# A graph network and attention kernel: the last sigmoid by the hyperbolic tangent, with its sum on another engine

## The chip, the cores and the metric

The kernel runs on one core of one Trainium2 chip. A core has five engines with a queue each, which run side by side and wait for one another by semaphores: TensorE (PE, matrix products, with its weight loads shown as PEld), VectorE (DVE), ScalarE (ACT), GpSimd (POOL) and SyncE (SP), which here only issues transfers. Within an engine the instructions run in the order in which they stand. The metric is the time of one execution on the device in microseconds (us); lower is better.

## The reference

The input x has 128 graphs of 128 nodes with 256 features, adj one weight matrix of 128 x 128 for each graph. Two layers follow, each behind a layer norm and a rectifier. Layer 0 is a graph product with a bias; layer 1 is attention with eight heads whose logits are sums of a q and a k, one number for each node and head:

```python
h = jnp.maximum(_layernorm(x, axis=-1), 0.0)
x = x + (adj @ (h @ weight) + bias)            # layer 0
h = jnp.maximum(_layernorm(x, axis=-1), 0.0)
logits = q + jnp.swapaxes(k, -1, -2)           # q, k = (h @ fc_w + fc_b) @ q_w, k_w
masked = jax.nn.leaky_relu(logits + (1.0 - adj) * NEG, negative_slope=0.01)
attn = jax.nn.softmax(masked, axis=-1)
out = (attn @ feat_proj) @ fp_w + fp_b + h     # heads side by side
x = x + jax.nn.sigmoid(out)                    # layer 1
```

All is in fp32. Two identities stand behind the change: sigmoid(z) = 0.5 tanh(z / 2) + 0.5, and a layer norm takes away any constant that is added to all features of a node.

## The kernel before

The 128 graphs are taken in 32 groups of 4. The nodes lie on the 128 partitions; a tile of a group's features is 128 x 1024. A loop over the groups has 44 slots each. In every slot PE gets one piece of work, by a fixed list of 11 (ORDER, L595) that is gone through once for each of the group's four units (two pairs of graphs, two halves of the heads): `aggregate` (L561) multiplies attention with features into PSUM, and `multiply` (L599) multiplies seven sums and differences of the unit before, f0 to f6, with weights that hold fc_w and fp_w together. `take` (L572) makes f0 to f6: f0, f1 and f3 are copies on ACT (L581, L589, L583), f4 and f6 sums on DVE (L585, L586), f5 and f2 differences on POOL (L587, L590). `combine` (L617) adds the products up into the tile z on DVE.

All other work is put into the slots by the list PLAN (L673), written out by hand: a slot, a group relative to the loop's (-1 is the group before, 1 the next), a function. Since every engine has a queue in that order, PLAN sets what stands in front of what. The functions that the change and the prediction touch:

- The attention of the next group: `masked` (slots 0, 5, 12) spreads k over a tile and adds the mask on DVE (L489, L497); `leaky` is eight ACT instructions for each graph (L510), `head_max` a reduction on DVE (L518), `exps` eight ACT instructions with sums (L526), `normal` a reciprocal on DVE (L534) and the product with it on POOL (L535); `move` issues SP's transfers (L546) that exchange blocks of 32 partitions, and `turn` transposes within the blocks on DVE (L553).
- `make_qk` (slot 24) computes q and k of the group after next on PE (L453) and adds their bias on DVE (L461). `turn_qk` (slot 27) transposes them on PE (L467), copies k and q out on DVE (L469, L471) and issues k to memory on SP (L473); `load_k` (slot 34) brings it back on all partitions (L478).
- Layer 0 of the group three ahead: `n1_stats` (slot 28) and `n1_apply` (slot 25) are its norm on DVE and ACT (L285, L319); `add_b0` (slot 29) adds the bias to x on POOL (L337), after `n1_apply` has read it; `first_a` and `first_b` (slots 35 to 40) are its products, and `first_b` adds x in two halves on DVE into the tile x1 (L390), on which `n2_stats` follow.
- The end of the group before: `residual_a` and `residual_b` add h on POOL (L648, L653), `sigmoid` (slot 28) runs on ACT, `finish` (slot 29) adds x1 on POOL, `store` (slot 34) issues the result on SP.

ACT has its functions in tables. Prelu, exp, the rectifier and copies run with one table here, sigmoid with another; the loads between them carry the line of the instruction that needs them.

Of the kernel before, what the change touches and what calls it, by code (L numbers as in the profile page):

```python
# [10 lines left out]
AF = mybir.ActivationFunctionType  # L11
ALU = mybir.AluOpType
# [16 lines left out]
def gnn_then_gat_kernel(  # L29
# [16 lines left out]
    nc = tc.nc  # L46
# [38 lines left out]
    nc.sync.dma_start(w0_sb, w0.rearrange("(c p) o -> p c o", p=P))  # L85
    b0_bc = const.tile([P, D], FP, name="b0_bc")
    nc.sync.dma_start(b0_bc, b0.partition_broadcast(P))
    fpb_j = const.tile([P, D], FP, name="fpb_j")


# [559 lines left out]
    def residual_b(s, pair):  # L650
        for b in range(2 * pair, 2 * pair + 2):
            z = s["z"][:, b].rearrange("p (c j q) -> p j c q", j=NB, q=Q)
            nc.gpsimd.tensor_tensor(z, z, s["h2"][:, b], ALU.add)  # L653

    def sigmoid(s, b0, nb):
        z = s["z"][:, b0 : b0 + nb]
        nc.scalar.activation(z, z, AF.Sigmoid)  # L657

    def finish(s, b0, nb):
        bs = slice(b0, b0 + nb)  # L660
        nc.gpsimd.tensor_tensor(s["z"][:, bs], s["z"][:, bs], s["x1"][:, bs], ALU.add)  # L661

    def store(s, b0, nb):
        bs = slice(b0, b0 + nb)
# [55 lines left out]
        (25, 3, n1_apply, 1),  # L720
        (27, "u", combine, 1, 4),
        (28, "u", take, 2, 1, 0),
        (27, 2, turn_qk),
        (28, 1, move, 0, range(8, 16)),
        (28, 1, normal, 3),
        (28, 3, turn_blocks),
        (28, 4, n1_stats, 0),
        (28, 4, n1_stats, 1),
        (28, -1, sigmoid, 0, GB),
        (29, -1, finish, 0, GB),  # L730
        (29, 3, add_b0),
        (30, 1, move, 1, range(6)),
# [173 lines left out]
    for g in range(NG):  # L906
        cur = groups[g]
        cur["z"] = pool["un"].tile([P, GB, D], FP, name="z", tag="z")
        last = units[-1]
        units = [{"s": cur, "pair": i // 2, "half": i % 2, "f": {}} for i in range(4)]  # L910
        for slot in range(4 * len(ORDER)):
            n, i = divmod(slot, len(ORDER))
            o = ORDER[i]
            if isinstance(o, tuple):
                aggregate(units[n], o[1], o[2])
            elif n or last:
                multiply(units[n - 1] if n else last, o)
            if g == 0:
                for at_, f, *args in FIRST_PLAN:
                    if at_ == slot:  # L920
                        f(*args)
            for at_, who, f, *args in PLAN:
                if at_ != slot or (g == 0 and f in LATE):
                    continue
                if who == "u":
                    u = last if args[0] < 0 else units[args[0]]
                    if u:
                        f(u, *args[1:])
                elif g + who in range(NG):
                    f(groups[g + who], *args)  # L930
            if g == NG - 1 and slot == 33:
                sigmoid(cur, 0, 2)
            if g == NG - 1 and slot == 35:
                finish(cur, 0, 2)
                store(cur, 0, 2)
    for o in ORDER:
        if not isinstance(o, tuple):
            multiply(units[3], o)
            combine(units[3], o)
    residual_b(cur, 1)  # L940
    sigmoid(cur, 2, 2)
    finish(cur, 2, 2)
    store(cur, 2, 2)

# [30 lines left out]
```

## Time and profile before

| | us |
|---|---|
| median of 3 runs | 1575.77 (1575.29 to 1577.64) |
| the profiled execution, its own time | 1576.38 |
| its span, first to last instruction | 1574.2 |

| engine | busy us | share of the span |
|---|---|---|
| PE | 1509.0 | 96% |
| DVE | 1228.9 | 78% |
| ACT | 1173.8 | 75% |
| POOL | 984.0 | 63% |

| group of instructions | count | mean us of one |
|---|---|---|
| table loads at L657 (sigmoid) | 30 | 1.283 |
| table loads at L526 (exp) | 30 | 1.283 |
| L657 ACT, sigmoid of a group | 31 | 1.057 |
| L661 POOL, the sum with x1 of a group | 31 | 2.377 |
| L337 POOL, the sum of x and the bias | 32 | 2.360 |
| L390 DVE, x1 by halves | 64 | 0.690 |
| L467 PE, the turn of q and k | 32 | 0.33 |

The profile is one execution. A span is the time from the first to the last instruction on the core; the execution's own time has some 2 us around it. Busy time of PE is modelled, since products overlap; where PE is concerned, starts of instructions are the surer measure. A timeline lists instructions in order of time with their start and length, and in brackets the idle time before one and the instruction that ended it.

### The profile page before, as it was taken

Reading aid. Unit: us, or ns where it says so; the run is one execution under the profiler, and the core shown is the slowest. Engines: PE = TensorE matmul, PEld = TensorE weight load, DVE = VectorE, ACT = ScalarE, POOL = GpSimd, SP = SyncE. Lnnn points to the kernel's source line nnn. Section 1 sums busy time; section 2 is a strip of 40 time slices with the busy share of each in tenths; the row PEclk is TensorE's granted clock in tenths of the full one; section 3 lists DMA queues with packets and bytes.
Section 4 is the critical chain, followed back from the end, with each engine's and each line's share of the span. In section 5 each row is a group of like instructions: output and inputs, shape, how many; then the busy total and the mean of one; then the engine's idle time right before and its main releaser. Section 6 shows DMA issues by size and latency. Waiting matters only on the chain.

```text
span 1574.2 us, 30745 instructions
## 1 busy us (share of the span) xinstructions
PE 1509.0 (96%) x9953; PEld 1213.2 (77%) x9953; DVE 1228.9 (78%) x2253; ACT 1173.8 (75%) x3889; POOL 984.0 (63%) x724
## 2 busy tenths in 40 slices
PE   7786999999999999999999999999999999999997
PEld 7565877887777878777777877777877777778776
DVE  5676778887777888777888877788887778887762
ACT  3683788777778877777987777897777789777751
POOL 3163766666676666676666667666666766666664
PEclk7888999999999999999999999999999999999999
DMA  5132434434444443444444344444434444433320
GB/s 181 34 88 63 104 84 97 94 90 88 101 93 97 95 93 78 102 104 90 97 93 95 80 102 105 87 98 92 94 82 101 107 83 98 92 78 80 73 68 27
DMA packets 259689, 142.07 MB, mean 90 GB/s; under 512 B 174901, under 2 KB 226505, under 8 KB 259273
## 3 DMA queue, kind: packets, MB, share of 16 engines
q1 hardware_dynamic: 259288, 139.79, 39.7%
q8 instruction: 78, 1.28, 0.4%
q14 instruction: 83, 0.67, 0.2%
q10 hardware_dynamic: 240, 0.33, 0.1%
HBM read 39.86 MB, written 17.30 MB: 36 GB/s over the span
## 4 chain that ended last, share of the span: by engine, by line
ACT 44%; PE 23%; DVE 16%; SPq 9%; issue 4%; DMA 2%; POOL 2%; ACTq 0%; POOLq 0%; DVEq 0%
ACT attn L526 18%; PE acc L609 11%; ACT attn L510 10%; SPq L546 6%; DVE attn L497 6%; ACT h L319 6%; PE x_ps L383 5%; PE g_ps L564 5%; DVE attn L489 5%; ACT f L589 2%; ACT L657 2%; ACT L526 2%; SPq L426 2%; ACT z L657 2%; DVE st L285 1%
## 5 line engine op out<-in xcount | busy, mean ns | idle before, releaser
L609 PEld LDWEIGHTS acc<-wts,f 128*128 128x128 f32 x7168 | 889.6, 192 | 281.2 <-issue 181.7
L609 PE MATMUL acc<-wts,f 128*128 128x128 f32 x7168 | 897.9, 276 | 23.8 <-DVE z L625 12.9
L564 PE MATMUL g_ps<-attnT,h 128*128 128x512 f32 x1024 | 530.1, 600 | 5.3 <-DVE attnT L553 3.3
L526 ACT ACTIVATE attn<-attn,nmax 128x128 f32<-128x128 f32 x1024 | 397.3, 396 | 0.4
L587 POOL TENSOR_TENSOR f<-f,f 128x512 f32<-128x512 f32 x128 | 163.2, 1275 | 286.7 <-DVE f L585 284.4
L510 ACT ACTIVATE attn<-attn,q 128x128 f32<-128x128 f32 x1024 | 312.9, 391 | 34.4 <-DVE attn L497 27.1
L535 POOL TENSOR_TENSOR attn<-attn,total 128x1024 f32<-128x1024 f32 x128 | 245.1, 1915 | 140.8 <-DVE total L534 140.8
L589 ACT COPY f<-g_ps 128x512 f32<-128x512 f32 x128 | 73.3, 572 | 241.1 <-PE g_ps L564 241.1
L518 DVE TENSOR_REDUCE nmax<-attn 128x8 f32<-128x1024 f32 x128 | 154.0, 1204 | 64.1 <-ACT attn L510 63.9
L526 ACT ACTIVATION_READ_ACCUMULATOR attn<-attn,nmax 128x1 f32 x1024 | 199.3, 195 | 0.0
L497 DVE TENSOR_TENSOR attn<-attn,mask 128x1024 f32<-128x1024 f32 x128 | 186.4, 1456 | 4.5
L590 POOL TENSOR_TENSOR f<-f,f 128x512 f32<-128x512 f32 x128 | 180.5, 1410 | 6.5 <-ACT f L589 3.9
L553 DVE STREAM_TRANSPOSE attnT<-attnB 128x1024 f32<-128x1024 f32 x128 | 153.3, 1218 | 39.7 <-DMA attnB<-attn 34.7
L489 DVE STREAM_TRANSPOSE attn<-kq 128x1024 f32<-128x1024 f32 x128 | 157.2, 1228 | 15.9 <-DMA kq<-k_mem 15.6
L564 PEld LDWEIGHTS g_ps<-attnT,h 128*128 128x128 f32 x1024 | 157.6, 194 | 13.8 <-issue 9.6
L383 PE MATMUL x_ps<-w_sb,ahT 128*128 128x256 f32 x512 | 124.2, 387 | 0.0
L585 DVE TENSOR_TENSOR f<-g_ps,f 128x512 f32<-128x512 f32 x128 | 87.1, 681 | 47.3 <-POOL attn L535 38.9
L661 POOL TENSOR_TENSOR z<-z,x 128x1024 f32<-128x1024 f32 (+1 forms) x33 | 76.2, 2310 | 56.3 <-ACT z L657 56.3
L653 POOL TENSOR_TENSOR z<-z,h 128x256 f32<-128x256 f32 x128 | 90.7, 731 | 23.3 <-DVE z L625 22.7
L581 ACT COPY f<-g_ps 128x512 f32<-128x512 f32 x128 | 74.0, 578 | 40.7 <-PE g_ps L564 39.6
L383 PEld LDWEIGHTS x_ps<-w_sb,ahT 128*128 128x128 f32 x512 | 93.5, 192 | 11.6 <-issue 0.7
L586 DVE TENSOR_TENSOR f<-f,g_ps 128x512 f32<-128x512 f32 x128 | 86.5, 676 | 0.0
(93 smaller groups left out, 1356.8 us busy)
## 6 DMA issues: line engine op xcount, KB each, us to landing
attnB<-attn SPq DMA_DIRECT2D x1019, 64.0 KB, 2.0
xg<-in_x_dram SPq DMA_DIRECT2D x32, 512.0 KB, 4.0
out_dram<-z SPq DMA_DIRECT2D x31, 512.0 KB, 3.1
h2B<-h SPq DMA_DIRECT2D x480, 32.0 KB, 1.9
ag<-in_adj_dram SPq DMA_DIRECT2D x32, 256.0 KB, 4.5
agB<-in_adj_dram SPq DMA_DIRECT2D x120, 64.0 KB, 4.5
fcw<-in_L_gnn_fc_w_dram SPq DMA_DIRECT2D x2, 1024.0 KB, 6.9
fpw<-in_L_gnn_fp_w_dram SPq DMA_DIRECT2D x1, 2048.0 KB, 14.1
```

The source lines that it names most:

```text
L383: nc.tensor.matmul(op[:, bb, :], lhsT=s["ahT"][:, 2 * b2 + bb, c, :], rhs=w0_sb[:, c, :], start=(c == 0), stop=(c == NC - 1),)
L489: nc.vector.transpose(s["a", b // 2][:, :, b % 2], s["kq"][:, :, b].unsqueeze(3).to_broadcast([P, NB, H, Q]),)
L497: nc.vector.tensor_tensor(a, a, s["mask"][:, b, :] .rearrange("p (j c) -> p j c", c=Q) .unsqueeze(2) .to_broadcast([P, NB, H, Q]), ALU.add,)
L510: nc.scalar.activation(a[:, :, h, :], a[:, :, h, :], AF.Prelu, bias=s["q"][:, b, h : h + 1], alpha=0.01,)
L518: nc.vector.tensor_reduce(nmax, a.rearrange("p j h c -> p h j c"), AX.XY, ALU.max, negate=True)
L526: nc.scalar.activation(a[:, :, h, :], a[:, :, h, :], AF.Exp, bias=s["nmax", b][:, h : h + 1], accum_out=s["total", b][:, h : h + 1],)
L535: nc.gpsimd.tensor_tensor(a, a, total.unsqueeze(1).unsqueeze(3).to_broadcast([P, NB, H, Q]), ALU.mult)
L553: nc.vector.transpose(aT.rearrange("p h (i r) -> p i h r", r=Q), s["ab", b // 2][:, :, b % 2])
L564: nc.tensor.matmul(u["g", b, c], lhsT=s["h2"][:, 2 * pair + b].rearrange("p j c q -> p (j c q)")[:, ts(c, P)], rhs=s["aT", 2 * pair + b][: ...
L587: nc.gpsimd.tensor_tensor(new(5), f[4], f[0], ALU.subtract)
L590: nc.gpsimd.tensor_tensor(new(2), f[1], f[5], ALU.subtract)
L609: nc.tensor.matmul(acc[:, slot, :], lhsT=u["f"][m][:, h, :], rhs=wt[m][:, half * HU + h, :], start=(half == 0 and h == 0 and m in FIRST), ...
```

## The change

Sigmoid becomes a hyperbolic tangent of half its argument. Its half factor is applied where x1 is added, in one instruction with two operations, which stands on DVE instead of POOL. Its half summand is added once, at the start, to the bias of layer 0, on POOL: so x1 is larger by 0.5 everywhere, the norm of layer 1 takes that away again, and the last sum has it. In PLAN, `turn_qk` goes from slot 27 to slot 28 and stands there behind `take`, so on PE behind the aggregation of slot 28.

```diff
     b0_bc = const.tile([P, D], FP, name="b0_bc")
     nc.sync.dma_start(b0_bc, b0.partition_broadcast(P))
+    nc.gpsimd.tensor_scalar(b0_bc, b0_bc, 0.5, None, ALU.add)
...
     def sigmoid(s, b0, nb):
         z = s["z"][:, b0 : b0 + nb]
-        nc.scalar.activation(z, z, AF.Sigmoid)
+        nc.scalar.activation(z, z, AF.Tanh, scale=0.5)
 
     def finish(s, b0, nb):
         bs = slice(b0, b0 + nb)
-        nc.gpsimd.tensor_tensor(s["z"][:, bs], s["z"][:, bs], s["x1"][:, bs], ALU.add)
+        nc.vector.scalar_tensor_tensor(
+            s["z"][:, bs], s["z"][:, bs], 0.5, s["x1"][:, bs], ALU.mult, ALU.add
+        )
...
         (27, "u", combine, 1, 4),
         (28, "u", take, 2, 1, 0),
-        (27, 2, turn_qk),
+        (28, 2, turn_qk),
         (28, 1, move, 0, range(8, 16)),
```

The SP, PE and ACT queues keep their order but for that step of PE and the table loads, which follow from the functions; DVE has one instruction more for each group, behind `n1_stats` and ahead of `combine`.

## The prediction

> **What bounds the kernel now.** I read the page's busy shares first, then the chain of work that ended last, then each engine's timeline in one middle period, 698 to 745 us. The page:
>
> ```profile
> PE 1509.0 (96%) x9953; PEld 1213.2 (77%) x9953; DVE 1228.9 (78%) x2253; ACT 1173.8 (75%) x3889; POOL 984.0 (63%) x724
> ACT 44%; PE 23%; DVE 16%; SPq 9%; issue 4%; DMA 2%; POOL 2%; ACTq 0%; POOLq 0%; DVEq 0%
> ```
>
> PE is nearly full, yet the chain runs mostly over ACT: one loop through ACT, PE and DVE sets the period. The chain in order of time, from the end of the exps:
>
> ```profile
> 734.33 1.28 ACT L657
> 735.62 1.06 ACT z L657
> 736.68 0.48 ACT f L589
> 737.21 1.16 PE acc L609 x8
> 738.37 1.81 PE x_ps L383 x8
> ...
> 744.59 0.70 DVE x L390
> ```
>
> The unnamed 1.28 us is a table load; behind it wait the sigmoid, the copy of f1 and PE's product. At 744.59 the second x1 add closes the loop. The same add stands at 698.47 and 744.59, a period of 46.12. From the add at 190.82 to that at 1436.50, both in the DVE timeline, are 27 periods: 46.14 each.
>
> How full is PE? Start to start without a wait, a period has 28 products of 0.893 (16 pieces take 1.785), 16 aggregations of 0.86, first_a 1.78, first_b 1.76 twice, the qk product 0.60 and the turn of qk 0.17: 44.8. So 1.3 us are gaps: about 0.7 round the wait for f1, 0.3 before the turn of qk, 0.3 round the qk product (waiting for h2T from DVE). The timelines of DVE, of POOL and of SP (start, length, instruction, idle time before it) at the period's end:
>
> ```profile
> 736.05 0.63 DVE L625 TENSOR_TENSOR z<-w,v 128x256 f32<-128x256 f32 x2
> 737.92 2.37 DVE L553 STREAM_TRANSPOSE attnT<-attnB 128x1024 f32<-128x1024 f32 x2 [1.25 <-DMA attnB<-attn]
> 741.47 0.69 DVE L390 TENSOR_TENSOR x<-x_ps,xg 128x512 f32<-128x512 f32 x1 [1.18 <-POOL xg L337]
> ```
>
> ```profile
> 736.76 2.36 POOL L661 TENSOR_TENSOR z<-z,x 128x1024 f32<-128x1024 f32 x1 [1.96 <-ACT z L657]
> 739.07 2.36 POOL L337 TENSOR_TENSOR xg<-xg,b_bc 128x1024 f32<-128x1024 f32 x1
> ```
>
> ```profile
> 730.70 0.51 SPq L473 DMA_DIRECT2D k_mem<-k  x1
> 731.26 8.74 SPq L546 DMA_DIRECT2D attnB<-attn  x14
> ```
>
> DVE waits for a transfer before L553, whose eighth move SP issues behind k_mem, and then for POOL's add_b0, which is queued behind the old finish. From L553 to the second add DVE needs 744.59 - 737.92 = 6.67, 1.22 of it the gap before L390; the rest is 5.45.
>
> **What the Trainium skill says.** "ScalarE: Activation LUTs", section Table sets, puts tanh into the set of exp; sigmoid has its own. Section What ACT_TABLE_LOAD costs gives 2.66 us a switch, drain included. The trace shows less: 1.28 for the load, and with the drained gap before it 1.41 (L589 at 710.96 to the exps at 712.84 is 1.88, against 0.47 after other copies). I use 1.41. "SBUF — State Buffer", section SBUF: two separate sides, says that a DVE instruction with two SBUF inputs and a GpSimd one hold a shared port exclusively, and the loser blocks. The trace agrees, on DVE and on POOL:
>
> ```profile
> 704.28 2.26 DVE L497 TENSOR_TENSOR attn<-attn,mask 128x1024 f32<-128x1024 f32 x1
> ...
> 1439.89 2.13 DVE L497 TENSOR_TENSOR attn<-attn,mask 128x1024 f32<-128x1024 f32 x1
> ```
>
> ```profile
> 704.18 1.28 POOL L648 TENSOR_TENSOR h<-h,fpb_j 128x512 f32<-128x512 f32 x1
> ...
> 1439.67 1.27 POOL L590 TENSOR_TENSOR f<-f,f 128x512 f32<-128x512 f32 x1
> 1440.90 2.25 POOL L648 TENSOR_TENSOR h<-h,fpb_j 128x512 f32<-128x512 f32 x1
> ```
>
> L497 takes 1.23 alone and ends 1.08 after POOL's instruction; at 1440.9 it went ahead of POOL's next one, which then ended 1.13 after it.
>
> **The change part by part.**
>
> Table loads. The page's L657 and L526 groups have 30 loads each; the changed program as built has 2 loads in all, before 61. So ACT runs 1.41 earlier from the first exps of a period on, and 2.81 earlier after the tanh. "ScalarE activation tables", section What a function is on this engine, says that the same operands cost the same whatever the table, so the tanh takes sigmoid's 1.06.
>
> The new finish. 128x1024 fp32 with two SBUF inputs: L497, the same size, takes 1.23. The only sizeable scalar_tensor_tensor is L248, 256 elements with a column operand, 0.485 median; the 768 elements more cost 0.80 between L625's 256 (0.42) and L497's 1024 (1.23), so 1.29. "Vector Engine (DVE) Microarchitecture Reference", Points that are easy to get wrong, says that this form with two fp32 SBUF inputs runs at half rate, about 2.3 here; L248 speaks against it: at that slope 256 elements at half rate are already 0.53. I take 1.23; the ends are 1.2 and 2.3. It leaves POOL (2.36) and joins DVE.
>
> Now one period, anchored at the add at 698.47. DVE is busy without a wait until 723.17, and nothing there changes. Then:
> 1. ACT's exps of block 0 start at 711.43 (712.84), the copy of f3 at 728.81 (730.22), so DVE's L585, which waits for it, at 729.47 (730.88).
> 2. POOL's normal 3, behind its L587, starts at 731.47 (732.88). The old finish is no longer behind it, n1_apply ends near 732.9, so add_b0 runs 733.34 to 735.70 (it ended at 741.43).
> 3. The tanh runs 732.81 to 733.87. DVE's n1_stats end 1.41 earlier, at 733.88: the new finish is not kept waiting by ACT, but add_b0 took the port half a microsecond before. So it starts when add_b0 ends and is over 1.08 later, at 736.78. Behind it in DVE's queue stand combine, L553 and the x1 adds.
> 4. combine: L641 at 736.70 (735.29), the z adds at 737.46; POOL's L590, held back by the finish, has the port until 736.78 + 1.13 = 737.91; the adds end near 738.39, as at 714.09, where they end 0.49 after L590.
> 5. L553 at 738.35 (737.92), and without the wait for add_b0 the second add 5.45 later, at 743.80 (744.59). Period 45.33: 0.79 less.
>
> So of 2.81 saved on ACT only 0.79 stays: the two DVE waits (1.25 and 1.18), which covered the finish, are used up.
>
> The turn of q and k. Now behind the next aggregation on PE and behind L585 and L586 on DVE. PE's 0.3 wait for L461 goes; but with ACT earlier, L461 ends at 725.35, before PE's old place (726.5), so the wait would go anyway. Its cost: k is ready at 730.83 (729.45), SP reaches k_mem at 730.70, so k_mem, 14 moves and load_k go out 0.23 later and L553's data at 738.15: hidden under DVE's 738.35, with 0.2 to spare. SP's order is unchanged. In the last period with a turn of qk, SP is there at 1468.22 and k comes at 1469.1: 0.9 late, and the spread at 1482.62 waits for it.
>
> The half. One POOL instruction on 256 elements, about 0.35, behind the bias's landing at about 7.0; the next work needed from POOL, at 7.97, waits for DVE: nothing. The shifted x1 changes no instruction.
>
> **The sum.** 27 periods x 0.79 = -21.3. First sigmoid period (168 to 190): PE has no gap there, nothing. End: the late k +0.9; PE's wait before 1514.60 -0.24; the last finish 0.69 for 1.26, -0.57: +0.1. From the profiled execution's 1576.38: 1555.2. The median of the runs shown is 0.6 lower: 1554.6.
>
> **Rivals.**
> - *The finish meets no lock* (add_b0 later, or the lock not applying). Then DVE is ready before its data, L553 starts at 738.15, the period is 45.13; PE's floor with the gap round qk left is 45.1. -27 x 1.0: 1549. For it: POOL is 0.55 ahead only.
> - *Heavier blocking*: the finish or the adds lose another 0.3 on DVE (a dearer instruction, a second blocked add): period 45.65, 1563.
> - *POOL goes first*: L590 takes the port ahead of the waiting finish. The finish then ends at 738.01, L553 starts at 739.28, the second add stands at 744.73: period 46.26, 1580, slower. It decides once L553 starts after 739.14. Against it: at 1440.9 DVE won. A half-rate finish would give 1584 the same way.
> - *No gain*: another wait (moves, kq) holds L553 at about 739.1. SP's waits leave it 1 us of room: 1576.
> - The naive sum, 30 x 2.81 = 84 us, can't be: PE's 44.8 a period allows 27 x 1.3 = 36, 1540 at best.
>
> **How the numbers follow.** Chances: forecast 0.50, no lock 0.22, heavier 0.16, POOL first or half rate 0.07, no gain 0.05. 0.2% (3 us) is about what a measurement can tell from no change. Faster: 0.50 + 0.22 + 0.16 = 0.88; same 0.05; slower 0.07. The range, 1546 to 1569, holds the first three cases with a few microseconds either side. I predict 1554.6 us.
>
> **What would show it.** Two table loads; x1 adds 45.3 apart; the finish (L664 there) about 2.9 long on DVE with add_b0 beside it; no POOL wait before L390; POOL in the chain. A period of 45.1 means no lock; a DMA wait before L553 means that SP, with the later k_mem, has taken over; a wait for the tanh before the finish would break step 3.

## The result, and the profile after

| | before | after |
|---|---|---|
| median, 4 runs each on one chip, us | 1575.53 (1573.83 to 1577.64) | 1555.84 (1552.82 to 1556.21) |
| ratio, 95% interval | | 0.987 (0.985 to 0.989) |
| profiled execution, us | 1576.38 | 1552.82 |
| span of it, us | 1574.2 | 1550.9 |

The kernel became 1.3% faster. The forecast was 1554.6 us, 1.2 us below the median. The profiled execution of after is the shortest of its four, so the sums below are made within the two spans, which differ by 23.4 us:

| stretch, by the second x1 add of each period ("the add" below) in the DVE timelines | before | after | difference |
|---|---|---|---|
| start to the add that opens the 27 periods | 190.82 | 190.55 | -0.3 |
| 27 periods | 1245.7 | 1223.6 | -22.1 |
| last of these adds to the end of the span | 137.7 | 136.7 | -1.0 |

The mean period went from 46.14 to 45.32 us. The page of after, busy time and then the shares of the chain that ended last:

```profile
PE 1494.5 (96%) x9953; PEld 1209.9 (78%) x9953; DVE 1312.8 (85%) x2286; ACT 1098.5 (71%) x3830; POOL 938.3 (61%) x692
ACT 33%; DVE 31%; SPq 11%; PE 9%; issue 6%; DMA 6%; POOL 3%; DVEq 0%; ACTq 0%; POOLq 0%
```

ACT lost 75 us of busy time, 59 table loads of 1.283 each, and a fourth of its share of the chain. DVE gained 84 us of busy time and twice the share. That is more than 33 sums of 1.23 us would add, and the groups of DVE by shape show why (count, then busy us in all and mean ns of one, then the idle time before them):

```profile
L554 DVE STREAM_TRANSPOSE attnT<-attnB 128x1024 f32<-128x1024 f32 x128 | 153.1, 1215 | 9.7 <-DMA attnB<-attn 6.2 <-issue 3.3
L664 DVE SCALAR_TENSOR_TENSOR z<-z,x 128x1024 f32<-128x1024 f32 x31 | 88.7, 2862 | 3.5 <-ACT z L660 3.5
L391 DVE TENSOR_TENSOR x<-x_ps,xg 128x512 f32<-128x512 f32 x64 | 42.6, 668 | 9.9 <-PE x_ps L384 9.9
```

The new finish lasts 2.86 us a group, more than twice L497's 1.23. L391 (L390 before) no longer waits for POOL at all. And the wait of L554 for its transfer, 34.7 us in 27 places before, is down to 6.2 (the view puts 3.3 more down to "issue", 5.0 before). One period of after, from the x1 add at 1323.96 to the one at 1369.06, on DVE, POOL and SP (start, length, instruction, idle time before it):

```profile
1323.96 0.68 DVE L391 TENSOR_TENSOR x<-x_ps,xg 128x512 f32<-128x512 f32 x1
...
1354.96 0.69 DVE L586 TENSOR_TENSOR f<-g_ps,f 128x512 f32<-128x512 f32 x1 [1.53 <-issue]
...
1359.37 2.92 DVE L664 SCALAR_TENSOR_TENSOR z<-z,x 128x1024 f32<-128x1024 f32 x1
1362.21 0.28 DVE L642 COPY p<-acc 128x128 f32<-128x128 f32 x1
...
1362.98 0.92 DVE L626 TENSOR_TENSOR z<-w,v 128x256 f32<-128x256 f32 x2
1363.82 2.36 DVE L554 STREAM_TRANSPOSE attnT<-attnB 128x1024 f32<-128x1024 f32 x2
1366.11 0.65 DVE L391 TENSOR_TENSOR x<-x_ps,xg 128x512 f32<-128x512 f32 x1
...
1369.06 0.68 DVE L391 TENSOR_TENSOR x<-x_ps,xg 128x512 f32<-128x512 f32 x1
```

```profile
1358.83 2.37 POOL L338 TENSOR_TENSOR xg<-xg,b_bc 128x1024 f32<-128x1024 f32 x1
1361.15 2.26 POOL L591 TENSOR_TENSOR f<-f,f 128x512 f32<-128x512 f32 x1
```

```profile
1350.67 5.64 SPq L547 DMA_DIRECT2D attnB<-attn  x8
1356.41 0.53 SPq L474 DMA_DIRECT2D k_mem<-k  x1
1356.98 8.74 SPq L547 DMA_DIRECT2D attnB<-attn  x14
```

The finish starts 0.54 behind add_b0 (L338), is held until it ends (at 1361.20), and is over 1.09 later, ahead of L591, which in turn ends 1.12 behind the finish. From 1359.37 to the add DVE has no wait. This period is 45.10 long, and 17 of the 27 are between 45.07 and 45.19; these are called clean below. The other ten reach 46.92, and a long one looks like this on DVE and SP:

```profile
1093.00 2.37 DVE L554 STREAM_TRANSPOSE attnT<-attnB 128x1024 f32<-128x1024 f32 x2 [0.86 <-issue]
```

```profile
1078.96 5.01 SPq L547 DMA_DIRECT2D attnB<-attn  x8
1084.62 0.36 SPq L474 DMA_DIRECT2D k_mem<-k  x1
1085.02 9.43 SPq L547 DMA_DIRECT2D attnB<-attn  x14
```

SP's moves end at 1083.97, and it then stands 0.65 before k_mem, because k is not there: `turn_qk` also copies k on DVE, and this copy now stands there behind L586 and L587. Of the moves behind k_mem, L554 needs the first eight. SP issues the eighth in its place, at 1089.37, but it lands only 3.35 later, at 1092.72, where the median of the 27 periods is 2.04; L554 starts 0.28 behind the landing. The 14 moves take 9.43 instead of 8.74 because the tenth took 1.28, at 1090.64, and that is not in front of the landing. The period is 46.04 long.

In all ten long periods L554 starts 0.12 to 0.28 behind the last landing of its 16 moves. In six of them one of the eight issues behind k_mem was slow (1.29 to 1.78 instead of 0.59), in one an issue ahead of k_mem (1.68), and in three, this one among them, the issues were even and the eighth move's landing took 2.95 to 3.65. These three make up about half of what the ten periods are longer. The DMA view of 1089.3 to 1092.8 shows what else was under way (queue, kind: packets, MB, share of the 16 DMA engines):

```profile
q1 hardware_dynamic: 218, 0.32, 40.0%
q8 instruction: 1, 0.02, 2.2%
```

One packet of another queue, which the trace marks as instruction, was moved in this time. The same view of the clean period above, 1356 to 1364, has none. The last section counts how often the two go together.

### The profile page after: what moved, and what is told of

Its sections match the earlier page's. It is cut to its first block, busy times and chain, and to the rows that moved or that the text cites. A ratio compares the mean times of both kernels' runs of the same rounds, so it can differ in the third digit from the quotient of the medians.

```text
span 1550.9 us, 30658 instructions
## 1 busy us (share of the span) xinstructions
PE 1494.5 (96%) x9953; PEld 1209.9 (78%) x9953; DVE 1312.8 (85%) x2286; ACT 1098.5 (71%) x3830; POOL 938.3 (61%) x692
## 3 DMA queue, kind: packets, MB, share of 16 engines
q1 hardware_dynamic: 259288, 139.79, 40.4%
q8 instruction: 78, 1.28, 0.4%
HBM read 39.86 MB, written 17.30 MB: 37 GB/s over the span
## 4 chain that ended last, share of the span: by engine, by line
ACT 33%; DVE 31%; SPq 11%; PE 9%; issue 6%; DMA 6%; POOL 3%; DVEq 0%; ACTq 0%; POOLq 0%
ACT attn L527 14%; ACT attn L511 11%; SPq L547 9%; DVE attn L498 7%; DVE attn L490 5%; PE acc L610 4%; ACT h L320 4%; DMA attnB<-attn 4%; DVE st L286 4%; DVE attnT L554 3%; DVE f L586 2%; DVE x L391 2%; PE g_ps L565 2%; DVE f L587 2%; POOL attn L536 2%
## 5 line engine op out<-in xcount | busy, mean ns | idle before, releaser
L588 POOL TENSOR_TENSOR f<-f,f 128x512 f32<-128x512 f32 x128 | 163.4, 1277 | 356.3 <-DVE f L586 356.2
L511 ACT ACTIVATE attn<-attn,q 128x128 f32<-128x128 f32 x1024 | 313.0, 392 | 42.0 <-DVE attn L498 22.1
L591 POOL TENSOR_TENSOR f<-f,f 128x512 f32<-128x512 f32 x128 | 209.3, 1635 | 7.8 <-ACT f L590 5.2
L498 DVE TENSOR_TENSOR attn<-attn,mask 128x1024 f32<-128x1024 f32 x128 | 186.4, 1456 | 4.5
L519 DVE TENSOR_REDUCE nmax<-attn 128x8 f32<-128x1024 f32 x128 | 153.9, 1203 | 23.4 <-ACT attn L511 23.3
L554 DVE STREAM_TRANSPOSE attnT<-attnB 128x1024 f32<-128x1024 f32 x128 | 153.1, 1215 | 9.7 <-DMA attnB<-attn 6.2
L586 DVE TENSOR_TENSOR f<-g_ps,f 128x512 f32<-128x512 f32 x128 | 87.0, 680 | 50.8 <-issue 24.5
L654 POOL TENSOR_TENSOR z<-z,h 128x256 f32<-128x256 f32 x128 | 90.7, 730 | 40.5 <-DVE z L626 39.9
L664 DVE SCALAR_TENSOR_TENSOR z<-z,x 128x1024 f32<-128x1024 f32 (+1 forms) x33 | 90.1, 2730 | 7.9 <-ACT z L660 7.9
L587 DVE TENSOR_TENSOR f<-f,g_ps 128x512 f32<-128x512 f32 x128 | 86.4, 675 | 0.0
```

The costliest lines, as they stand in the source:

```text
L498: nc.vector.tensor_tensor(a, a, s["mask"][:, b, :] .rearrange("p (j c) -> p j c", c=Q) .unsqueeze(2) .to_broadcast([P, NB, H, Q]), ALU.add,)
L511: nc.scalar.activation(a[:, :, h, :], a[:, :, h, :], AF.Prelu, bias=s["q"][:, b, h : h + 1], alpha=0.01,)
L519: nc.vector.tensor_reduce(nmax, a.rearrange("p j h c -> p h j c"), AX.XY, ALU.max, negate=True)
L554: nc.vector.transpose(aT.rearrange("p h (i r) -> p i h r", r=Q), s["ab", b // 2][:, :, b % 2])
L588: nc.gpsimd.tensor_tensor(new(5), f[4], f[0], ALU.subtract)
L591: nc.gpsimd.tensor_tensor(new(2), f[1], f[5], ALU.subtract)
```

## The experiments

The theory after the result: the gain comes from the table loads; how much of it stays is set by what stands in front of L554 and of the x1 adds, which is the lock of add_b0 on the finish, as forecast, or the transfers; and the later turn of q and k costs more than the forecast's nothing. The rivals are that the lock is not what makes the finish long (a half-rate instruction), that the finish would do as well on POOL, and that the moved step is free. Three sets were run, each on one chip with nine runs of the kernel before, to which its ratios are: first the changed kernel again, the step taken back, the sum on POOL and add_b0 in slot 31 (before: 1574.93 us); then the step alone, the finish alone, add_b0 in slot 32 and the last version (1575.58); then the remaining three (1574.08).

### The changed kernel again, and its moved step taken back

The first is the changed kernel without an edit.

> The changed kernel once more, on the chip of the other three, so that they are compared with it there. 1555.8 us, between 1552.5 and 1557; x1 adds 45.3 apart on average, most of them 45.1 apart and some ten of 27 longer, where the transfers before L554 are late.

Measured: 1555.81 us, ratio 0.988 (0.986 to 0.989), mean period 45.31. The second puts the step back:

```diff
-        (28, 2, turn_qk),
+        (27, 2, turn_qk),
```

> The change with turn_qk left in slot 27, all else as changed. Theory: the step took no wait away that ACT's earlier exps had not taken already, and made k_mem 0.6 us later on SP, so that every slow issue behind it delays L554. Back in slot 27, k is ready 1.4 us earlier, SP does not wait for it, nearly all periods are 45.1, and the last turn of q and k saves up to 0.9: about 1549 us, 1546 to 1552. Rival A, the long periods have nothing to do with SP: as changed, 1556. Rival B, the step itself frees PE of its 0.3 us wait in each period: 1563.

Measured: 1550.38 us, ratio 0.985 (0.983 to 0.986), mean period 45.19. The same kernel was run once more, in the third set:

> The changed kernel with turn_qk back in slot 27, again, beside the next run on one chip. 1550.4 us (1548 to 1553), mean distance of the second x1 adds 45.2 us.

It took 1550.56 us, ratio 0.984 (0.982 to 0.986), mean period 45.18. So the moved step costs about 5 us of what the change gains. The clean periods are as long as in after (45.08 to 45.10); what changes is the long ones: the mean stands 0.10 over the clean period here and 0.23 in after. On SP of the kernel with the step taken back, in one of its periods:

```profile
1350.52 5.89 SPq L547 DMA_DIRECT2D attnB<-attn  x8
1356.51 0.53 SPq L474 DMA_DIRECT2D k_mem<-k  x1
```

k_mem is issued 0.1 behind the last move. That holds in all its periods, and in all of before. In after the median idle time of SP at this place is 0.54, and k_mem goes out 32.42 behind the add instead of 31.87 in before (medians of 28).

### The moved step alone

The kernel before, with only the step moved, the other way about:

```diff
-        (27, 2, turn_qk),
+        (28, 2, turn_qk),
```

> The kernel before with turn_qk in slot 28 alone. Theory: PE's wait of 0.3 us goes, but it was no part of the loop; k is copied behind L585 and L586, at 33.7 us of a period instead of 31.0, SP waits 2 us for it, and the transfers that L553 needs land near 41.1 to 41.5: period 46.3 to 46.6, 1584 us, 1577 to 1592. Rival, that the step pays by itself: 27 times 0.3, 1567.

Measured: 1585.71 us, ratio 1.006 (1.005 to 1.007), mean period 46.49. SP and DVE of one of its periods:

```profile
1378.10 5.49 SPq L546 DMA_DIRECT2D attnB<-attn  x8
1385.21 0.36 SPq L473 DMA_DIRECT2D k_mem<-k  x1
```

```profile
1392.28 2.37 DVE L553 STREAM_TRANSPOSE attnT<-attnB 128x1024 f32<-128x1024 f32 x2 [2.70 <-DMA attnB<-attn]
```

SP stands 1.62 before k_mem (median of all periods 1.94), and L553 waits 2.70 for its data instead of 1.25. This shows the mechanism at more than three times its size in after: with the table loads still in front of f3, L585 is 1.41 later than in after, k stands behind it, and everything SP issues for the next group stands behind k.

### The new finish alone

The kernel before, with the sum on DVE by the new instruction, but a factor of 1.0, and the sigmoid and its tables kept:

```diff
-        nc.gpsimd.tensor_tensor(s["z"][:, bs], s["z"][:, bs], s["x1"][:, bs], ALU.add)
+        nc.vector.scalar_tensor_tensor(
+            s["z"][:, bs], s["z"][:, bs], 1.0, s["x1"][:, bs], ALU.mult, ALU.add
+        )
```

> The kernel before with the last sum on DVE alone (the two-operation form with a factor of one; sigmoid and its tables, the bias and the plan as before). Theory: nothing is won without the table loads. The sum comes behind the sigmoid at 38.3 us of a period and behind add_b0's hold on the port (to 38.7), ends at 39.8, the z adds end behind L591 near 41.4, L554 starts there, 1.7 later than its transfers, the period is 46.6: 1587 us, 1581 to 1591. Rival, that moving the sum off POOL is worth something by itself (the 1.18 us that DVE waited for add_b0 in each period): 1550 to 1570.

Measured: 1584.96 us, ratio 1.006 (1.005 to 1.007), all periods 46.47 to 46.51. Its DVE:

```profile
1391.27 1.48 DVE L661 SCALAR_TENSOR_TENSOR z<-z,x 128x1024 f32<-128x1024 f32 x1 [1.33 <-ACT z L657]
...
1394.29 2.36 DVE L553 STREAM_TRANSPOSE attnT<-attnB 128x1024 f32<-128x1024 f32 x2
```

With the table load in front of it the sigmoid is late, and now DVE waits for it, with combine, L553 and the x1 adds queued behind. By itself the finish on DVE loses; it needs the earlier tanh.

### The tanh, with the last sum on POOL

The third part by itself, in the place where the step stands in after, and then with it taken back too. In both the factor of a half is left out, since POOL makes a plain sum here:

```diff
-        nc.vector.scalar_tensor_tensor(
-            s["z"][:, bs], s["z"][:, bs], 0.5, s["x1"][:, bs], ALU.mult, ALU.add
-        )
+        nc.gpsimd.tensor_tensor(s["z"][:, bs], s["z"][:, bs], s["x1"][:, bs], ALU.add)
```

> The change with the last sum left on POOL, as a plain sum: the factor of a half is left out of it, nothing else. Theory: what is won is won by the table loads alone. POOL's sum runs from about 35.5 to 37.8 us of a period and add_b0 to 40.2, before L391 needs it (41.7); DVE is free before its transfers, L554 starts with them near 39.4, and PE's 45.1 is the period, with 0.4 us of room for late transfers: 1551 us, 1548 to 1554. Rival, that the sum on DVE is what took the wait for add_b0 away: that wait of about 1.2 us is back and the period at 46 or more: 1574.

> tanh and the shifted bias alone: turn_qk in slot 27 and the last sum on POOL as a plain sum; the factor of a half is left out of the sum. Theory: with the sum on POOL the z adds of combine, blocked by POOL twice, set L554 at 40.4 behind the add, not the transfers, so an earlier k changes nothing: 1564 us (1561 to 1567), as with turn_qk in slot 28. Rival: the late k costs here too what it costs with the sum on DVE, about 5 us: 1559 us (1557 to 1561).

Measured: 1564.73 us, ratio 0.994 (0.992 to 0.995), with the step in slot 28; 1563.25, ratio 0.992 (0.991 to 0.994), with it in slot 27; mean periods 45.63 in both. The first expectation failed, and so did its rival: there is no wait for POOL before L391. What happens, with the step in slot 28, on DVE and POOL:

```profile
1369.22 4.29 DVE L626 TENSOR_TENSOR z<-w,v 128x256 f32<-128x256 f32 x2
1373.44 2.36 DVE L554 STREAM_TRANSPOSE attnT<-attnB 128x1024 f32<-128x1024 f32 x2
```

```profile
1368.52 2.36 POOL L664 TENSOR_TENSOR z<-z,x 128x1024 f32<-128x1024 f32 x1 [0.54 <-ACT z L660]
1370.83 2.53 POOL L338 TENSOR_TENSOR xg<-xg,b_bc 128x1024 f32<-128x1024 f32 x1
```

The two small z adds of combine, 0.63 alone, now meet POOL's sum and add_b0 one after the other, and take 4.29. In the gap between them POOL got the port back. L554 starts 40.4 behind the add instead of 39.9. The second expectation was made with that known and held: where DVE's lock sets L554, an earlier k gives nothing that these runs can tell.

### The lock taken away

If add_b0 is what makes the finish long, moving it makes the finish short. First behind `take` in slot 31:

```diff
-        (29, 3, add_b0),
         (30, 1, move, 1, range(6)),
         (31, "u", take, 2, 0, 1),
+        (31, 3, add_b0),
```

> The change with add_b0 behind take in slot 31 instead of in slot 29, so that POOL's first instruction on the port comes after DVE has begun the last sum; no work more or less. Theory (a lock for the whole instruction): the sum takes 1.23 us, not 2.9, DVE is free before the transfers as in c, period 45.1 to 45.2: 1551 us, 1548 to 1554. Rival, the instruction itself is slow (half rate or more): it still takes 2.3 to 2.9, and the time is that of the changed kernel, 1556.

Measured: 1561.76 us, ratio 0.992 (0.991 to 0.994), mean period 45.67. DVE and POOL:

```profile
1368.32 1.22 DVE L664 SCALAR_TENSOR_TENSOR z<-z,x 128x1024 f32<-128x1024 f32 x1
...
1370.23 3.08 DVE L626 TENSOR_TENSOR z<-w,v 128x256 f32<-128x256 f32 x2
1373.24 2.36 DVE L554 STREAM_TRANSPOSE attnT<-attnB 128x1024 f32<-128x1024 f32 x2
```

```profile
1368.89 1.77 POOL L591 TENSOR_TENSOR f<-f,f 128x512 f32<-128x512 f32 x1 [1.07 <-ACT f L590]
1370.63 2.53 POOL L338 TENSOR_TENSOR xg<-xg,b_bc 128x1024 f32<-128x1024 f32 x1
```

The instruction needs 1.22 when nothing holds the port: the half rate is refuted and the lock confirmed. The time was missed by 11 us, because the lock only went to the next pair of instructions, the z adds, 3.08 instead of 0.92. So add_b0 goes behind those and POOL's sum after them, `residual_b`:

```diff
-        (29, 3, add_b0),
...
         (32, 0, residual_b, 0),
+        (32, 3, add_b0),
```

> The change with add_b0 behind residual_b in slot 32, so that on POOL it comes after the z adds of combine. In the run with add_b0 in slot 31 the last sum took 1.22, but the two z adds behind it took 3.08 instead of 0.63, since POOL's L591 and add_b0 came between them. Theory (the lock moved from the sum to the z adds there): now both are short, 1.22 and about 1.1 (L591 alone), L554 starts with its transfers, add_b0 ends near 42.0 us of a period, L391 waits for it a little, and the period is 45.0 to 45.2: 1553 us, 1550 to 1556, some 9 less than with slot 31. Rival, that add_b0 is simply too late in both: L391 waits longer than in slot 31 and the time is 1562 or more.

Measured: 1554.44 us, ratio 0.987 (0.985 to 0.988), mean period 45.35. The finish takes 1.22 and the z adds 0.92, and L554 waits for its transfer in 26 places, 42.6 us in all. So most of the time that the lock took is now a wait for the transfers. Would it help with k in time? The same, with `turn_qk` in slot 27:

> turn_qk in slot 27 and add_b0 behind residual_b in slot 32. Theory: with k in time PE bounds the clean period (44.8 of work and the gap before qk), so taking the lock away from the finish and thereby making DVE ready about 1.7 us earlier gains little: clean periods 45.0 to 45.1, some of the long ones gone, 1548 us (1545 to 1551). Rival: DVE still bounds even with k in time; then the 1.7 us go on until the transfers stop them, L554 starts near 39.3 behind the add and the period goes to 44.8: 1540 us (1537 to 1543).

Measured: 1548.73 us, ratio 0.984 (0.982 to 0.985), mean period 45.21. The lines of DVE's waits (us in all, places, longest):

```profile
DVE attnT L554 <- DMA attnB<-attn: 39.9, 28, 2.6
...
DVE x L391 <- POOL xg L338: 10.4, 14, 2.7
```

L554 waits for its transfer in every period, and in 14 of them the x1 add then waits for the add_b0 that was moved. In its new place add_b0 ends 42.04 behind the add, and the first x1 add starts at 42.07 to 42.09 in most clean periods, hardly earlier than with the lock (median 42.14 with the step taken back). So this run takes the lock away but puts another wait in nearly the same place, and what the lock alone costs with k in time it does not show. Against the kernel with the step taken back (1550.56 in the same set) no gain is shown: the intervals overlap and the mean periods are 45.21 and 45.18. The lock forecast for the finish is real, but once the tables are gone it hides a wait of nearly the same length for the moves: DVE is ready for L554 1.7 earlier here, and L554 starts 0.16 earlier (medians 39.69 and 39.85 behind the add).

### A version that beats both

The kernel with the step taken back, and on POOL `residual_a` put before the second norm's last steps. Before this L498 (L497 of before), 128x1024 on DVE, took 2.26 beside POOL's L649:

```diff
-        (28, 2, turn_qk),
+        (27, 2, turn_qk),
...
-        (41, 3, rdev_both),
+        (42, 0, residual_a, 1),
+        (42, 3, rdev_both),
         (42, "u", take, 3, 0, 1),
-        (43, 0, residual_a, 1),
```

> The change with turn_qk in slot 27 and with residual_a of the second pair in front of POOL's power (both in slot 42, behind the aggregation that reads its tile). Theory: the second L498 of a period no longer waits for the port (2.26 to 1.23), all of DVE's loop comes 1.0 us earlier, the 0.3 us gap of PE at the qk product goes, and with more than 1 us of room for late transfers PE alone sets the period, 44.8: 1541 us, 1538 to 1545. Rival, the loop is not DVE's: as with turn_qk in slot 27 alone, 1550.

Measured: 1546.89 us, ratio 0.982 (0.980 to 0.983), mean period 45.13, clean periods 44.95 (ten of the 27). It has the lowest median here, with 29 us off, but 6 us over what was expected; its interval overlaps those of the two runs of the third set that come closest (0.982 to 0.985 and 0.982 to 0.986). Its DVE, POOL and PE show where two parts of the gain went:

```profile
1069.90 1.25 DVE L431 STREAM_TRANSPOSE h2T<-h2B 128x1024 f32<-128x1024 f32 x1 [0.30 <-issue]
...
1093.60 1.10 DVE L298 TENSOR_SCALAR rstd<-mv 128x4 f32<-128x4 f32 x2
...
1098.30 1.22 DVE L498 TENSOR_TENSOR attn<-attn,mask 128x1024 f32<-128x1024 f32 x1
```

```profile
1093.34 1.26 POOL L649 TENSOR_TENSOR h<-h,fpb_j 128x512 f32<-128x512 f32 x1 [0.81 <-PE g_ps L565]
```

```profile
1071.20 0.67 PE L454 MATMUL qk_ps<-h2T,wqk 128*32 128x128 f32 x16 [0.43 <-DVE h2T L431]
```

L498 is short now, but the pair at L298, 0.24 for both alone, stands beside L649 in its place and takes 1.10 here, 0.86 in the median. And L431 has caught up with the transfers of h2, so that PE still has its gap before the product for q and k. How much each of the two costs was not separated.

### The parts together

| finish on | tables | turn_qk in slot | us | ratio to before |
|---|---|---|---|---|
| POOL | sigmoid | 28 | 1585.71 | 1.006 |
| DVE | sigmoid | 27 | 1584.96 | 1.006 |
| POOL | tanh | 27 | 1563.25 | 0.992 |
| POOL | tanh | 28 | 1564.73 | 0.994 |
| DVE | tanh | 27 | 1550.38 and 1550.56 | 0.985 and 0.984 |
| DVE | tanh | 28 (the change) | 1555.84 and 1555.81 | 0.987 and 0.988 |

Parts don't add up: the finish on DVE costs 9 us with the sigmoid and gains 13 with the tanh (1563.25 to 1550.56, same set). The step costs 10 us without the tanh and 5 with tanh and DVE; with tanh and POOL the two runs, of different sets, differ by 1.5 us and their intervals overlap.

## Why the prediction was right, and where it was not

**Table loads (right).** Two are left, and the exps run 1.41 earlier: L586 starts 31.00 behind the add, the forecast's own number (729.47 - 698.47). The tanh takes sigmoid's 1.06, as "ScalarE activation tables" of the Trainium skill, What a function is on this engine, had it.

**Steps 2 to 4, the lock (right).** add_b0 was forecast at 34.87 to 37.23 behind the add and stands at 34.87 to 37.24. The finish was to end at 38.31 and ends at 38.33, ahead of L591; the z adds were to end at 39.92 and end at 39.94. "POOL goes first" is refuted at this place by the trace, where L591 ends 1.12 behind the finish. So is the half rate, by the 1.22 us of two runs: the Trainium skill's "Vector Engine (DVE) Microarchitecture Reference", Points that are easy to get wrong, doesn't hold for this instruction. "SBUF — State Buffer", SBUF: two separate sides, says that whichever instruction starts first gets the shared port for its whole length. The traces shown here agree: add_b0 had started 0.54 before the finish. What it doesn't say decides this case: which of two that wait is next, and that a pair of short instructions can lose the port between them.

**Step 5 (a term too large).** L554 starts at 39.86, forecast 39.88; but from there the second add is 5.24 away, not 5.45. The 5.45 was taken from a period of before in which part of it was waiting, mostly for PE's products, and not work: between the two x1 adds lie 3.12 there (741.47 to 744.59) and 2.95 here (1366.11 to 1369.06). The clean period is 45.1, not 45.33: by this term alone the change would have given 27 x 0.24 = 6 us more.

**The turn of q and k (wrong in size).** The step that failed is "so k_mem, 14 moves and load_k go out 0.23 later and L553's data at 738.15: hidden under DVE's 738.35, with 0.2 to spare". The 0.23 was read off one period in which SP reached k_mem at 32.23 behind the add; the median is 31.87, and the delay 0.55. Where issues and landings are even, the data come in time all the same: the last landing is then at 39.2 behind the add, and L554 starts at 39.86. But the forecast took one even path, and where an issue or a landing is slow the later k leaves too little room for it: ten periods are longer, which is 0.23 on the mean of all 27, 6 us in all. With the step taken back 0.10 is left, so by the traces 3.5 of these 6 are the step's, and by the medians it cost 5; where the rest lies is open. In before the uneven transfers had no effect: periods are alike within 0.05 but for two. DVE's timeline there shows why, in two of them:

```profile
875.67 2.37 DVE L553 STREAM_TRANSPOSE attnT<-attnB 128x1024 f32<-128x1024 f32 x2 [0.66 <-DMA attnB<-attn]
879.82 0.69 DVE L390 TENSOR_TENSOR x<-x_ps,xg 128x512 f32<-128x512 f32 x1 [1.78 <-POOL xg L337]
```

```profile
923.08 2.37 DVE L553 STREAM_TRANSPOSE attnT<-attnB 128x1024 f32<-128x1024 f32 x2 [1.94 <-DMA attnB<-attn]
925.93 0.69 DVE L390 TENSOR_TENSOR x<-x_ps,xg 128x512 f32<-128x512 f32 x1 [0.48 <-POOL xg L337]
```

The longer DVE waits before L553, the shorter it waits for add_b0 behind it: in 25 of the 27 periods the two add up to 2.4. That was 1.2 us of room in the median period, and the change used it up.

So the two errors, of 6 us each and of opposite sign, cancel in the mean period: 45.32 measured, 45.33 forecast. The closeness of the total is partly luck.

**Head and end.** The head was forecast as unchanged and became 0.3 shorter; the end was forecast at +0.1 and became 1.0 shorter. Neither difference can be told from what one kernel varies by: in the two traces of the kernel with the step taken back the heads are 194.5 and 192.6 and the ends 137.6 and 136.3. The late k is there as forecast (SP stands 1.0 before the last k_mem, from 1445.77 to 1446.76).

**The rivals.** "The finish meets no lock" was given 1549 us and a period of 45.13; the run without the lock and with k in time took 1548.7, with clean periods of 45.08 and L554 waiting for its data, as that rival said. But with the lock and k in time the clean period is as long (1550.6 us in all), so the agreement doesn't tell the two apart. In the two runs with add_b0 in slot 32 its end holds the first x1 add; where the finish meets the lock, DVE has no wait from the finish to the add; and by its modelled end (44.95 behind the add) PE's last product would allow the second add only some 0.1 earlier. These limits, the moves and PE's own 44.8 with its gap before the product for q and k lie within 0.3 of one another, and which of them would remain if one were taken away is not settled.

## What to carry to other kernels

Before a wait is used up, ask what irregularity it has absorbed: 1.2 us of idle time on one engine made every period alike, and without it a step that comes half a microsecond late on a transfer queue cost a fifth of the gain that there was without it. Take a delay on a queue from the distribution over all periods, not from the one period that is open on the screen, and subtract the waits when a stretch of one timeline is carried over to another. Where two engines share a port, moving an instruction moves the blocked place: price the instructions that stand next to it, above all pairs of short ones, which can lose the port between them.

## What was not expected of the hardware

- Two short DVE instructions in a row lost the port once each: the z adds, 0.63 for both alone, took 4.29 beside two POOL sums and 3.08 beside one and the end of another, while a single long one (the finish) beside add_b0 and L591 lost only once.
- The lock shows on very small instructions: the pair at L298, 128x4 each, took 1.10 instead of 0.24 beside POOL's L649 (0.86 in the median of the last version's periods).
- SP's issues and the landings are not even, and the uneven ones go together with packets of 16 KB on queue q8 that the trace marks as instruction. In the 27 periods of after, all 50 issues of moves and of h2's transfers that took over 0.8 us overlap in time with such a packet; of the other 1245, 40 do. Of the 117 landings that took over 2.4 us, 101 overlap with one, and the other 16 with one of queue q14, marked the same; of the 855 shorter ones, 46 overlap with one of q8. In before it is the same for the issues: 42 of 42 against 48 of 1253. No run tested whether these packets hold the transfers up.
